# Attention in a two-layer kernel: inverse roots and inverse row sums as exponentials of logarithms

## The chip, the cores and the metric

The program runs on one core of a Trainium2 chip. The metric is the device time of one execution in microseconds. Three executions of the kernel before took 3812.17, 3815.10 and 3818.73 us; the median is 3815.1 us.

## The reference

The input x has 16 batches of 256 tokens with 256 channels. Two layers are added to it in turn. The first runs a shared and a routed feed-forward block, and then a lookup in product keys. The second runs a recurrent cell over the tokens (an LSTM), and then the block that this document is about: attention with 16 heads of 16 channels, and a mixture of 8 experts with two chosen for each token. Cut to this block:

```python
def _layernorm(x, g, b):
    m = jnp.mean(x, axis=-1, keepdims=True)
    v = jnp.mean(jnp.square(x - m), axis=-1, keepdims=True)
    return (x - m) * jax.lax.rsqrt(v + EPS) * g + b
h = _layernorm(x, ln1_g, ln1_b)
q, k, v = jnp.split(h @ w_qkv + b_qkv, 3, axis=-1)          # 16 heads of 16
attn = jax.nn.softmax(einsum('bqhd,bkhd->bhqk', q, k) / np.sqrt(DK), axis=-1)
x = x + einsum('bhqk,bkhd->bqhd', attn, v).reshape(B, S, D) @ w_o + b_o
h = _layernorm(x, ln2_g, ln2_b)
# logits = h @ gate_w + gate_b, the two largest, their softmax as weights,
# relu(h W1 + b1) W2 + b2 of the two experts, added to x with the weights
```

The change concerns three places in it: the inverse root of each of the two norms, and the division by the row sums of the softmax.

## The kernel before

Everything is computed in float32, with channels on the 128 partitions and tokens along the free axis. The attention stage begins at about 2523 us, after the recurrent cell, and works through the 16 batches one by one. A batch passes three generators, which hand over at each `yield`:

- `front(b)`: the first norm (`normed`, lines 1118 to 1140), then the products for queries and keys (L1156, bias and scale on ScalarE at L1159) and for values (L1167, L1169).
- `heads(b)`: four groups `c` of four heads. `largest` multiplies queries and keys (L1190), and takes each row's maximum on VectorE (L1197). `shift` transposes the maxima on TensorE (L1202) and adds them to the queries (L1203). `powers` multiplies again (L1190) and takes Exp on ScalarE (L1209, four of 128x512 for a group). `values` multiplies the powers with the values and with ones (L1220), so that the row sums come out beside the weighted sums; ScalarE copies both into `oT` (L1223).
- `ends(b)`: divides by the row sums (L1242 to L1247), applies the output projection (L1251) and the residual (L1253), runs the second norm (`normed`), adds and stores the sum (L1259 on GpSimd, L1260 a DMA issued by ScalarE's queue), computes the router's logits (L1267), the two choices and their weights (L1269 to L1293, one Exp at L1290), the tokens' rows (L1297 to L1307), their places (L1312 to L1323), four scatters by GpSimd's DMA (L1326), and the list of tiles (L1346 to L1380).

`normed` takes the mean and the variance by products with a matrix of 1/256 (L1122, L1131), so each partition holds the whole mean. In between, VectorE subtracts (L1124) and GpSimd squares (L1126). After the variance come the inverse root (L1133, L1134), the product with it (L1135), and gain and offset (L1137).

Beside them runs `experts()`: tiles of 128 tokens of one expert, 71 in all. A tile is loaded by SyncE (token rows, 1 MB of weights, two biases), transposed (L1413, L1415), multiplied (L1425, in two halves, relu alternately on VectorE at L1431 and ScalarE at L1429), multiplied again (L1438), weighted (L1443), and scattered by GpSimd (L1446). At one time a tile's second product stands between the transposition and the first product of the next.

The order is written out by hand in `drive` (line 1479): `heads(b)` has nine places. At each place one step of `heads(b)` is recorded, then the share of `ends(b - 1)` that falls to it (nine steps over nine places), of `front(b + 1)` (six steps), and of the expert tiles (three pieces to a tile; some 3.6 tiles to a batch once enough tokens have been routed, none in the first batches). After the last batch, `ends(15)` runs over 16 places between tiles, and then the remaining tiles. A layer below the kernel assigns buffers and waits and may move an instruction within its neighbourhood; each engine then runs its own queue in order. Two PSUM buffers (the pool `mm`) serve all of L1122, L1131, L1156, L1167, L1202, L1220, L1251, L1267, L1297 and the small products of the router, in turn. Four others hold the products L1190.

ScalarE keeps one set of function tables at a time. Where the next function is in another set, the build places a table load in front of it; the profile names it ACT_TABLE_LOAD, with the line of that function.

```python
        def drive(main, sides, tiles_from, tiles_to, places):
            a, z = tiles_from * PIECES, tiles_to * PIECES
            for k in range(places):
                steps(main, 1)
                for s, n in sides:
                    steps(s, (k + 1) * n // places - k * n // places)
                go(a + (z - a) * (k + 1) // places)
```

Of the kernel before, what the change touches and what calls it, by code (L numbers as in the profile page):

```python
# [11 lines left out]
AF = mybir.ActivationFunctionType  # L12
ALU = mybir.AluOpType
# [26 lines left out]
def bc(ap, axis, n):  # L40

    a = ap.unsqueeze(axis)
    shape = list(a.shape)
    shape[axis] = n
    return a.to_broadcast(shape)
# [116 lines left out]
def adaln_ffn_kernel(ctx: ExitStack, tc: tile.TileContext, i: dict, out: bass.AP):  # L162
    nc = tc.nc
# [15 lines left out]
    eps = const.tile([P, 1], F32, name="eps")  # L179
# [443 lines left out]
    with tc.tile_pool(name="cw", bufs=1) as cw:  # L623
# [5 lines left out]
        bias = cw.tile([P, 4 * D], F32, name="bias")  # L629
# [369 lines left out]
    QP = QC // 2  # L999
# [3 lines left out]
    with (  # L1003
# [58 lines left out]
        bias = fl.tile([P, 2, QP, 2], F32, name="bias")  # L1062
# [52 lines left out]
        def mm():  # L1115
            return pmm.tile([P, NTT, T], F32, name="mm", tag="mm")

        def normed(x, which, out):

            mean = mm()[:, 0]  # L1120
            for k in range(KC):
                nc.tensor.matmul(mean, ones_d, x[:, k], start=(k == 0), stop=(k == KC - 1))  # L1122
            h = fx.tile([P, KC, T], F32, name=f"h{which}", bufs=2 - which)
            nc.vector.tensor_tensor(h, x, bc(mean, 1, KC), ALU.subtract)  # L1124
            sq = fx.tile([P, KC, T], F32, name="sq", bufs=1)
            nc.gpsimd.tensor_tensor(sq, h, h, ALU.mult)  # L1126
            out.append(h)
            yield
            var = mm()[:, 0]
            for k in range(KC):  # L1130
                nc.tensor.matmul(var, ones_d, sq[:, k], start=(k == 0), stop=(k == KC - 1))  # L1131
            rs = fx.tile([P, T], F32, name="rs", bufs=1)
            nc.scalar.activation(rs, var, AF.Sqrt, bias=eps)  # L1133
            nc.vector.reciprocal(rs, rs)  # L1134
            nc.vector.tensor_tensor(h, h, bc(rs, 1, KC), ALU.mult)  # L1135
            for k in range(KC):
                nc.vector.tensor_scalar(  # L1137
                    h[:, k], h[:, k], lnw[:, 2 * which, k : k + 1], lnw[:, 2 * which + 1, k : k + 1], ALU.mult, ALU.add
                )
            yield  # L1140
# [3 lines left out]
        def front(b):  # L1144

            if b + 1 < B and b > 0:
                load_z(b + 1)
            o = []
            yield from normed(zs[b], 0, o)
            hn = o[0]  # L1150
            qk = qks[b] = fx.tile([P, 2, QC, T], F32, name="qk")
# [87 lines left out]
        def ends(b):  # L1239

            oT, z = outs[b], zs[b]
            rs = fx.tile([P, QP, T], F32, name="rsum", bufs=1)  # L1242
            on = fx.tile([P, QP, T], F32, name="on", bufs=1)
            for h in range(QP):
                nc.vector.reciprocal(rs[:, h], oT[:, h, 1])
                nc.gpsimd.tensor_tensor(on[:, h], oT[:, h, 0], rs[:, h], ALU.mult)
                yield  # L1247
            pw = mm()
            for d in range(KC):
                for k in range(QP):  # L1250
# [5 lines left out]
            yield  # L1256
            o = []
            yield from normed(z, 1, o)
            nc.gpsimd.tensor_tensor(x, x, z, ALU.add)  # L1259
            nc.scalar.dma_start(out=x3d[:, :, b * T : (b + 1) * T], in_=x)  # L1260
# [232 lines left out]
        for b in range(B):  # L1493
            sides = []
            if b:
                sides.append((ends(b - 1), 9))
            if b + 1 < B:
                sides.append((front(b + 1), 6))
            drive(heads(b), sides, planned(b - 1), planned(b), NPL)
        drive(ends(B - 1), [], planned(B - 1), allowed(B - 1), 16)  # L1500
        attn.close()
        pools["first"] = final.enter_context(tc.tile_pool(name="ep2", bufs=2, space=PSUM))
# [102 lines left out]
```

## Time and profile before

| what | us |
|---|---|
| median of three executions | 3815.1 |
| the profiled execution, its own time | 3815.34 |
| its span, from first to last instruction | 3813.4 |
| PE (TensorE, products) busy | 3575.2 |
| DVE (VectorE) busy | 2311.3 |
| ACT (ScalarE) busy | 1278.5 |
| POOL (GpSimd) busy | 698.1 |
| attention stage, first norm to last routing | about 2533 to 3585 |
| inverse of the roots, L1134, 32 times | 56.0 |
| inverse of the row sums, L1245, 32 times | 55.9 |
| table loads at L1133, L1209 and L1290, 64 times | 82.2 |

How to read the lines shown further on: a line of a timeline gives the start, the duration (both in us), the engine, the source line, the operation, what it writes and reads, and in brackets how long the engine had been idle before it and what ended that. A line of groups gives the total busy time and the mean of one in ns, then the idle time before these instructions. PEld is the loading of weights into TensorE. The granted clock is the share of TensorE's full clock that it was given.

### The profile page before, as it was taken

Reading aid. Unit: us, or ns where it says so; the run is one execution under the profiler, and the core shown is the slowest. Engines: PE = TensorE matmul, PEld = TensorE weight load, DVE = VectorE, ACT = ScalarE, POOL = GpSimd, SP = SyncE. Lnnn points to the kernel's source line nnn. Section 1 sums busy time; section 2 is a strip of 40 time slices with the busy share of each in tenths; the row PEclk is TensorE's granted clock in tenths of the full one; section 3 lists DMA queues with packets and bytes.
Section 4 is the critical chain, followed back from the end, with each engine's and each line's share of the span. In section 5 each row is a group of like instructions: output and inputs, shape, how many; then the busy total and the mean of one; then the engine's idle time right before and its main releaser. Section 6 shows DMA issues by size and latency. Waiting matters only on the chain.

```text
span 3813.4 us, 74402 instructions
## 1 busy us (share of the span) xinstructions
PE 3575.2 (94%) x27672; PEld 2820.5 (74%) x27672; DVE 2311.3 (61%) x7704; ACT 1278.5 (34%) x3158; POOL 698.1 (18%) x1148
## 2 busy tenths in 40 slices
PE   7899879999999999999999999959999999999896
PEld 4377468888888888888888888825677777777796
DVE  3333378777777777877777777434554545554323
ACT  1133123333333333333333333323343433433221
POOL 3544310000000000000000100001222222222321
PEclk9999979999999999999999999968899999999997
DMA  6233521011111111011101111040133323232566
GB/s 227 93 106 104 163 34 29 15 34 21 34 21 29 26 29 34 15 34 21 34 18 32 21 32 25 19 127 17 55 98 99 109 86 114 93 113 87 177 225 215
DMA packets 423365, 273.15 MB, mean 72 GB/s; under 512 B 304800, under 2 KB 381472, under 8 KB 412384
## 3 DMA queue, kind: packets, MB, share of 16 engines
q1 hardware_dynamic: 397776, 208.21, 20.3%
q0 software_dynamic: 13344, 36.60, 2.6%
q10 hardware_dynamic: 11888, 23.60, 1.8%
q8 instruction: 223, 3.65, 0.4%
q14 instruction: 134, 1.10, 0.1%
HBM read 191.88 MB, written 76.44 MB: 70 GB/s over the span
## 4 chain that ended last, share of the span: by engine, by line
PE 81%; DVE 6%; DMA 6%; issue 3%; ACT 3%; POOL 2%; SPq 0%; DVEq 0%; ACTq 0%; POOLq 0%
PE acc L819 13%; PE po L810 12%; PE wp L794 12%; PE gp L887 8%; PE g L1438 6%; PE g L1425 5%; PE sc L1190 3%; PE mm L1220 3%; PE bp L843 3%; PE sp L708 3%; PE ph L517 2%; PE py L531 2%; DMA axd<-row,slot 1%; PE mm L1156 1%; PE mm L1251 1%
## 5 line engine op out<-in xcount | busy, mean ns | idle before, releaser
L819 PEld LDWEIGHTS acc<-ge,kout 128*128 128x128 f32 x4096 | 485.2, 192 | 73.8 <-issue 56.9
L810 PEld LDWEIGHTS po<-yt,kin 128*128 128x128 f32 x3840 | 460.9, 192 | 100.7 <-issue 100.7
L819 PE MATMUL acc<-ge,kout 128*128 128x128 f32 x4096 | 522.0, 279 | 2.9 <-DVE ge L816 2.9
L794 PEld LDWEIGHTS wp<-oh,ol 128*128 128x128 f32 x4096 | 494.3, 195 | 28.5 <-issue 24.2
L794 PE MATMUL wp<-oh,ol 128*128 128x64 f32 x4096 | 507.7, 274 | 7.0 <-DVE oh L791 4.0
L810 PE MATMUL po<-yt,kin 128*128 128x128 f32 x3840 | 508.6, 281 | 0.0
L907 POOL TENSOR_SCALAR zt<-hT 128x32 f32<-128x32 f32 x256 | 148.4, 580 | 1606.8 <-DVE hT L906 1439.0
L788 DVE TENSOR_TENSOR ol<-chosen,iota 128x1024 f32<-128x1024 f32 x256 | 315.4, 1232 | 106.2 <-PE wp L794 74.6
L887 PE MATMUL gp<-wh,hT 128*32 128x256 f32 x4096 | 326.9, 393 | 27.7 <-DVE hT L906 18.4
L797 ACT COPY wts<-wp 128x256 f32<-128x256 f32 x512 | 166.6, 375 | 449.9 <-PE wp L794 449.9
L1438 PE MATMUL g<-mw,hT 128*128 x1136 | 280.9, 402 | 9.0 <-ACT hT L1429 3.9
L1425 PE MATMUL g<-xT,w 128*128 128x128 f32 x2272 | 273.6, 276 | 0.0
L1425 PEld LDWEIGHTS g<-xT,w 128*128 128x128 f32 x2272 | 268.8, 192 | 4.4 <-issue 0.3
L1438 PEld LDWEIGHTS g<-mw,hT 128*128 128x128 f32 x1136 | 224.1, 203 | 46.8 <-ACT xT L1415 7.8
L1429 ACT ACTIVATE hT<-g,b 128x128 f32<-128x128 f32 x284 | 104.3, 368 | 437.1 <-DVE hT L1431 371.6
L816 DVE TENSOR_TENSOR ge<-ge,wts 128x512 f32<-128x512 f32 x256 | 175.8, 687 | 88.9 <-ACT ge L815 81.4
L893 ACT ACTIVATE g<-gp 128x192 f32<-128x192 f32 x256 | 84.5, 330 | 424.5 <-PE gp L887 424.5
L815 ACT ACTIVATE ge<-po 128x512 f32<-128x512 f32 x256 | 152.7, 597 | 212.7 <-PE po L810 202.0
L887 PEld LDWEIGHTS gp<-wh,hT 128*32 128x32 f32 x4096 | 120.4, 110 | 127.4 <-issue 27.5
L1190 PE MATMUL sc<-qk 32*128 32x256 f32 x2048 | 199.8, 425 | 14.8 <-DVE npads L1197 10.3
L1431 DVE TENSOR_SCALAR hT<-g,b 128x128 f32<-128x128 f32 x284 | 96.5, 341 | 133.9 <-PE g L1425 82.8
L896 DVE SCALAR_TENSOR_TENSOR fc<-g,cell 128x64 f32<-128x64 f32 x256 | 58.1, 227 | 196.1 <-ACT g L893 194.1
(349 smaller groups left out, 5554.3 us busy)
## 6 DMA issues: line engine op xcount, KB each, us to landing
w<-in_mw SPq DMA_DIRECT2D x71, 1024.0 KB
xwd<-xw SPq DMA_DIRECT2D x64, 256.0 KB
xr<-xwd SPq DMA_DIRECT2D x256, 64.0 KB
xs<-axd SPq DMA_DIRECT2D x71, 129.0 KB
xs<-xsd SPq DMA_DIRECT2D x71, 129.0 KB
b<-in_b SPq DMA_DIRECT2D x71, 128.0 KB
r<-ayd SPq DMA_DIRECT2D x64, 128.0 KB
mw<-in_mw SPq DMA_DIRECT2D x8, 1024.0 KB
```

The lines of the kernel that those rows point to most:

```text
L788: nc.vector.tensor_tensor(ol, bc(c[:, 0, g : g + GT], 2, P), bc(iota, 1, GT), ALU.is_equal)
L794: nc.tensor.matmul(wp[:, t], ol[:, t, :], oh[:, t, :], start=True, stop=True)
L797: nc.scalar.copy(w[:, :, at : at + GT], wp[:, :, r, :].rearrange("p t c -> p c t"))
L810: nc.tensor.matmul(po[:, h, :].rearrange("p (b t) -> p b t", t=SPC), kin[:, k, (c + h) * P : (c + h + 1) * P], yu[:, k], start=(k == 0), s ...
L815: nc.scalar.activation(ge, po, AF.Gelu)
L816: nc.vector.tensor_tensor(ge, ge, w[:, c : c + CQ, :], ALU.mult)
L819: nc.tensor.matmul(acc[d], kout[:, c + h, d * P : (d + 1) * P], ge[:, h, :], start=(c + h == 0), stop=(c + h == NC - 1))
L887: nc.tensor.matmul(gp[j * CW : (j + 1) * CW], state["hT"][:, k, :], group(wh, k, j), start=False, stop=(k == KC - 1), skip_group_check=True,)
L907: nc.gpsimd.tensor_scalar(zt[:, :, :, t], hT[:, :, 0:B], 0.5, None, ALU.mult)
L1190: nc.tensor.matmul(s[j][:, t], qk[rows(j), w, c, t * P : (t + 1) * P], qk[rows(j), 1 - w, c, :], start=True, stop=True)
L1425: nc.tensor.matmul(ph[:, f], w1[n][:, k, at * P : (at + 1) * P], xT[n][:, k], start=(k == 0), stop=(k == KC - 1))
L1438: m = nc.tensor.matmul(acc, hT[n][:, f], mw2[:, bass.ds(e, 1), f].rearrange("p o d -> p (o d)"), start=(f == 0), stop=(f == NF - 1))
```

## The change

In `normed`, ScalarE's Sqrt of the variance and VectorE's reciprocal become a Ln and an Exp with scale -0.5, both on ScalarE. In `ends`, two rounds of a reciprocal on VectorE, a product on GpSimd and a `yield` become one Ln and one Exp with scale -1 over both halves on ScalarE, one product on VectorE, and one `yield`. So `ends` has eight steps where it had nine, while `drive` still deals them out as nine.

```diff
             rs = fx.tile([P, T], F32, name="rs", bufs=1)
-            nc.scalar.activation(rs, var, AF.Sqrt, bias=eps)
-            nc.vector.reciprocal(rs, rs)
+            nc.scalar.activation(rs, var, AF.Ln, bias=eps)
+            nc.scalar.activation(rs, rs, AF.Exp, scale=-0.5)
             nc.vector.tensor_tensor(h, h, bc(rs, 1, KC), ALU.mult)
...
             rs = fx.tile([P, QP, T], F32, name="rsum", bufs=1)
             on = fx.tile([P, QP, T], F32, name="on", bufs=1)
-            for h in range(QP):
-                nc.vector.reciprocal(rs[:, h], oT[:, h, 1])
-                nc.gpsimd.tensor_tensor(on[:, h], oT[:, h, 0], rs[:, h], ALU.mult)
-                yield
+            nc.scalar.activation(rs, oT[:, :, 1], AF.Ln)
+            nc.scalar.activation(rs, rs, AF.Exp, scale=-1.0)
+            nc.vector.tensor_tensor(on, oT[:, :, 0], rs, ALU.mult)
+            yield
             pw = mm()
```

## The prediction

> **What bounds the kernel now.** I read the page's busy row first, then the stages, the waits of the attention stage, and its timeline at the places where PE stood still. The page:
>
> ```profile
> PE 3575.2 (94%) x27672; PEld 2820.5 (74%) x27672; DVE 2311.3 (61%) x7704; ACT 1278.5 (34%) x3158; POOL 698.1 (18%) x1148
> ```
>
> PE is the bound of the program, with 238 us not busy. The changed lines run only from about 2523 us on. The stages by windows (columns: length, then busy us and count of PE, PEld, DVE, ACT, POOL, granted clock, DMA share, GB/s):
>
> ```profile
> 2600.00:2755.00 155.00, 143.92 (x1004) 93.05 (x1005) 80.06 (x208) 60.80 (x107) 29.95 (x51) 0.84 0.11 35
> 2755.00:3541.00 786.00, 740.26 (x6218) 590.73 (x6210) 411.49 (x1107) 306.94 (x625) 201.53 (x289) 0.96 0.31 101
> 3541.00:3600.00 59.00, 48.85 (x313) 43.61 (x306) 21.53 (x74) 12.58 (x31) 18.22 (x22) 0.91 0.47 158
> ```
>
> In the middle stage (twelve batches, with expert tiles between the heads) PE is 94% busy, DVE 52%, ACT 39%. So neither DVE time nor ACT time counts by itself; what counts is PE's 46 us of idling and what ends it. The waits, over 2720 to 3813 us (waiting line, releaser, us in total, times, longest):
>
> ```profile
> PE mm L1267 <- ACT hT L1429: 12.9, 11, 1.7
> PE mm L1202 <- ACT rs L1133: 10.6, 7, 3.5
> PE mm L1360 <- ACT hT L1429: 6.8, 8, 0.9
> ```
>
> L1267 (router logits) is put down to hT, but in the timeline it starts as the normalised h is ready: the last wait is the norm chain. One such place:
>
> ```profile
> 3042.73 1.28 ACT L1209 ACT_TABLE_LOAD   x1
> 3044.02 2.06 ACT L1209 ACTIVATE at<-sc 128x512 f32<-128x512 f32 x4
> ...
> 3046.10 1.28 ACT L1133 ACT_TABLE_LOAD   x1
> ...
> 3047.40 0.47 ACT L1133 ACTIVATE rs<-mm,eps 128x256 f32<-128x256 f32 x1
> ...
> 3047.91 1.75 DVE L1134 RECIPROCAL rs<-rs 128x256 f32<-128x256 f32 x1 [5.60 <-ACT rs L1133]
> ...
> 3047.93 0.44 PE L1202 MATMUL mm<-ident,npads 128*128 128x128 f32 x2 [1.09 <-ACT rs L1133]
> ...
> 3051.18 1.07 PE L1267 MATMUL mm<-w_wg,h 128*128 128x8 f32 x8 [1.74 <-ACT hT L1429]
> ...
> 3052.80 5.31 PE L1438 MATMUL g<-mw,hT 128*128 x16
> ```
>
> Read it as a chain: table load, four Exps, table load, Sqrt (which frees the PSUM buffer that L1202 needs), reciprocal, two DVE steps, logits. PE stands still 1.1 and 1.7 us, and the next L1438 takes 5.31 us where an unstalled one takes 3.62: the clock dropped. Listing PE's timeline from 2755 to 3541, eight batches are of this kind (B). They lose 24.8 us at L1202 and L1267, 6.8 us at L1360, and 14.9 us in slow L1438. Four (A, where L1438 lies between variance and logits) lose only 3.7 us at L1131 and 2.4 us at L1267.
>
> **The change, part by part.** The groups that it touches:
>
> ```profile
> L1134 DVE RECIPROCAL rs<-rs 128x256 f32<-128x256 f32 x32 | 56.0, 1749 | 75.5 <-ACT rs L1133 75.4
> L1245 DVE RECIPROCAL rsum<-oT 128x256 f32<-128x256 f32 x32 | 55.9, 1748 | 28.1 <-ACT oT L1223 28.1
> L1133 ACT ACT_TABLE_LOAD x32 | 41.1, 1283 | 0.6
> L1209 ACT ACT_TABLE_LOAD x19 | 24.4, 1283 | 32.1 <-PE sc L1190 21.9 <-issue 10.0
> L1290 ACT ACT_TABLE_LOAD x13 | 16.7, 1283 | 0.2
> L1133 ACT ACTIVATE rs<-mm,eps 128x256 f32<-128x256 f32 x32 | 15.2, 474 | 16.3 <-PE mm L1131 15.9
> ```
>
> *Engine time.* Removed: 64 reciprocals, 112 us of DVE, and 32 multiplies L1246, 23.5 us of POOL. Added to DVE: 16 multiplies of 128x512 at 0.69 us (row L1135), 11 us. ACT: Ln stands for Sqrt at 0.47. No row shows an Exp of 128x256 from SBUF; a copy of that size from PSUM takes 0.37 (L1415), and SBUF costs some 0.04 more (0.256 at L902 against 0.218 at L894), so between 0.37 and 0.47: I take 0.42, 32 times. Ln and Exp of 128x512: 0.605 (L1209) plus 0.04, between 0.60 and 0.70, I take 0.63, 32 times.
>
> *Table loads.* Here two rules of the Trainium skill speak. Its page "ScalarE: Activation LUTs", section "Table sets: the hidden batching unit", says that one set holds both ln and exp, so the pair needs one load; all the switches of this stage could then go. The built order of the changed kernel says otherwise: a load stands before every Ln and every Exp, 96 in the stage against 64 (32+19+13), and none is left at L1209 and L1290. I go by the built order: 32 x 1.283 = 41 us more on ACT. With one set the place 0 stall below would vanish and the time be about 3770. The same page, section "What ACT_TABLE_LOAD costs", gives about 2.66 us for a switch, a drain of 1.38 included. The rows show 1.28: the four Exps start at 3044.02, where the load from 3042.73 ends. By the page each pair would be 2.76 us longer, at two places in twelve batches 66 us, and the time about 3860. I take the row.
>
> Sum on ACT: 41 + 13 + 20 = 74 us, some 56 of it in the middle stage: 39% becomes 46%, still no bound.
>
> *Order.* Dropping one yield makes ends() eight steps instead of nine. Everything from L1251 on (output projection, z, second norm, logits, routing, four scatters L1326 on POOL, the tile list) comes one place earlier between the heads. Its DMAs: the load of x (SP, L1255) waits for its buffer, which the store L1260 frees; it is issued a place earlier and landed long before use. L1260 on ACT's queue now stands before two hT and the four Exps of the first head group, and waits for L1259 on POOL, which stands before both L1126. The tile list is earlier, which can only help the 5.8 us wait for xs at 3590.
>
> *Place 0, where a wait is added.* After the last values PE goes on as here:
>
> ```profile
> 3015.78 0.58 ACT L1223 COPY oT<-mm 128x512 f32<-128x512 f32 x1 [1.83 <-PE mm L1220]
> ...
> 3018.76 2.48 DVE L1197 TENSOR_REDUCE npads<-sc 128x2 f32<-128x512 f32 x4
> ...
> 3022.40 0.38 PE L1202 MATMUL mm<-ident,npads 128*128 128x128 f32 x2
> ```
>
> In the new DVE order the multiply L1246 stands before these four maxima, and waits for the second activation: oT ends 3016.36, load 3017.65, Ln 3018.3, load 3019.6, Exp 3020.2, multiply 3020.95, maxima 3023.45. L1202 could start at 3022.4 and waits 1.05 us. Behind L1246 on DVE stand the maxima and ys; for the maxima waits PE. If L1438 (3.6 us, the cover here) is missing, as in batches 1 to 3, it is 2.1 us. Next, z is ready 12.6 us after the values' end, L1259 at 13.9, so L1260 leaves ACT before the Exps, whose products end at 15.4: nothing late there.
>
> *The norm places.* PE's new order in B: variance of the front, L1425, L1438, maxima products, variance of ends (ends at 26.0 on the same scale), L1425 2.0, products 1.15, logits. On ACT the load is done before; Ln 26.5, load 27.8, Exp 28.25; DVE 0.69 and 0.73 with hand-over to 29.8. PE arrives at 29.15: 0.65 us of waiting. In A: variance ends at 22.3, but ACT first does the transposed tile and two hT (23.85), then load 25.15, Ln 25.65, load 26.95, Exp 27.4, DVE 28.95; PE arrives at 27.45 after L1438: 1.5 us. L1202 finds its buffer free in both, and L1360 now follows the values (3.6 us), so its wait goes.
>
> *Sum of the middle stage.* B: before 24.8 + 6.8 + 14.9 = 46.5, after 8 x (1.05 + 0.65) = 13.6: 33 less. A: before 6.1, after 4 x 2.55 = 10.2: 4 more. Of the slow-clock part I count half, since the new waits may drop the clock as well: 7.5 back. Net -33 + 4 + 7.5 = -22 us.
>
> *Batches 1 to 3* (no tiles between): by the same walk the first group of Exps comes 3.8 us later, but the last values end 4.4 us sooner, because the reciprocal that held L1203 (1.96 us of PE at 2694) is gone. Between +12 and -13 over the three; I take 0. *Tail:* the 1.8 us wait at 3566 for an hT behind Sqrt goes, one behind L1260 may come: between +2 and -8 with the xs wait; 0. *First norm:* load and Exp (1.70) replace the reciprocal (1.75): 0.
>
> The profiled execution has a span of 3813.4 and took 3815.3, beside a median of 3815.1. 3815 - 22 = **3793 us**.
>
> **The rivals.**
> 1. *ScalarE's chain sets the pace* (slower). L1246 ties DVE's queue to a chain of two loads on ACT ahead of the maxima, in 15 batches, and the clock drops after such waits. For it: L1202 has only 1.1 us of slack left over the maxima even now; in batches 1 to 3 it has none. Against it: DVE and ACT are half idle, and one L1438 covers most of the chain. Price: 15 x 2.4 = 36 us, with half of the gain left (-12): 3839. It decides once the wait per batch passes some 2 us, where the slow L1438 begins to be paid too.
> 2. *The stall only moves*: the norm chain has 4 engine steps before and after, two loads of 1.28 against load and reciprocal; if the earlier place gives no slack, only the 6.8 us at L1360 are saved and the 1.05 x 12 paid: 3815 to 3821, say 3817.
> 3. *The gain comes in full*: the slow clock goes wholly and batches 1 to 3 gain: 3815 - 29 - 13 = 3773.
>
> **How the numbers follow.** A measurement of this kernel tells 0.2% (7.6 us) from no change. Likeliest case and case 3 together 0.58 (its own range 3768 to 3808), case 2 0.12, case 1 0.30. The bounds of the unknown costs (batches 1 to 3 at +-12, tail, clock) make 3768 the low end; with case 1 at 3839 and its spread, 3848 the high end. Faster 0.60, same 0.09, slower 0.31.
>
> **What would show it.** 96 table loads of 1.28 us at L1133, L1134, L1244, L1245, none at L1209. A wait of about 1 us at L1202 for npads once a batch, in the place after L1167; waits of L1267 under 1.5 us; none at L1360; L1438 at 3.6 us after the logits. I am wrong if L1202 or L1251 wait over 2 us in place 0, if the loads take longer than 1.3 us, or if the Exps L1209 wait behind L1260.

## The result and the profile after

The changed kernel took a median of 3844.0 us (3841.5 to 3859.6) against 3815.1 us, a ratio of 1.0082 with a 95% interval of 1.0061 to 1.0104: slower by 29 us between the medians and by 31 us as the ratio. The forecast of 3793 us had the wrong sign; rival 1 had said 3839. The profiled execution has a span of 3841.7 us and took 3844.0.

The busy row of the changed kernel, then the last two of the stretches that the prediction showed of the kernel before (columns as there):

```profile
PE 3570.1 (93%) x27672; PEld 2817.2 (73%) x27672; DVE 2221.5 (58%) x7656; ACT 1350.2 (35%) x3254; POOL 673.5 (18%) x1116
```

```profile
2755.00:3541.00 786.00, 715.52 (x5996) 568.41 (x5993) 333.27 (x1020) 352.34 (x678) 176.87 (x256) 0.96 0.29 97
3541.00:3600.00 59.00, 54.91 (x477) 45.26 (x476) 21.57 (x81) 23.84 (x49) 15.32 (x23) 1.00 0.36 117
```

VectorE fell from 411 to 333 us in the middle stretch and ScalarE rose from 307 to 352, where I had worked out 56 us more (the stretch no longer cuts quite the same work; over the same eleven batches in each kernel, those of the table below, ScalarE goes from 287 to 337). PE, the bound, is busy for 91% of it, where it was 94%. In the last stretch it is busier than before (54.9 against 48.9): its wait for xs there fell from 5.8 to 2.6 us. Its waits from 2720 us on (waiting line, releaser, us in total, times, longest), to be set against the three waits shown of before:

```profile
PE g L1438 <- ACT xT L1415: 21.8, 14, 3.2
PE mm L1267 <- DVE h L1137: 15.2, 10, 2.0
...
PE g L1438 <- ACT hT L1429: 13.3, 5, 3.3
PE mm L1202 <- DVE npads L1197: 10.6, 11, 1.0
...
PE mm L1202 <- DVE where L1364: 8.8, 8, 1.7
```

L1360's wait is gone and L1202 no longer waits for rs, as predicted. In their place stand two waits of L1438, which the prediction did not have, a longer one of L1267, and two new ones of L1202: for the maxima (L1197), and for L1364, a step of the tile list on VectorE. The groups on ScalarE and VectorE that answer to those of before:

```profile
L1133 ACT ACT_TABLE_LOAD x32 | 41.1, 1283 | 36.3 <-PE mm L1131 33.3 <-DVE h L1135 2.6
L1134 ACT ACT_TABLE_LOAD x32 | 41.1, 1283 | 0.6
...
L1244 ACT ACT_TABLE_LOAD x16 | 20.5, 1283 | 0.3
...
L1134 ACT ACTIVATE rs<-rs 128x256 f32<-128x256 f32 x32 | 13.3, 416 | 0.4
...
L1246 DVE TENSOR_TENSOR on<-oT,rsum 128x512 f32<-128x512 f32 x16 | 11.1, 692 | 34.4 <-ACT rsum L1245 34.4
```

The sizes are those of the prediction (1.283, 0.416 and 0.692 us; Ln and Exp of 128x512 take 0.63). What it had not read is in the first row: the loads of L1133 stood idle 33 us for the variance, where in the row of before it is 0.6 in all. No load is left at L1209 and L1290.

One place of kind B, in order of time. PE stands still twice:

```profile
3055.30 1.28 ACT L1133 ACT_TABLE_LOAD   x1
...
3056.60 0.47 ACT L1133 ACTIVATE rs<-mm,eps 128x256 f32<-128x256 f32 x1
...
3057.09 1.28 ACT L1134 ACT_TABLE_LOAD   x1
...
3058.38 0.42 ACT L1134 ACTIVATE rs<-rs 128x256 f32<-128x256 f32 x1
3058.70 0.35 ACT L1415 COPY xT<-g 128x256 f32<-128x256 f32 x1
...
3059.11 5.41 PE L1438 MATMUL g<-mw,hT 128*128 x16 [2.60 <-ACT xT L1415]
...
3065.63 1.13 PE L1131 MATMUL mm<-sq,ones_d 128*128 128x256 f32 x4
...
3066.84 1.28 ACT L1133 ACT_TABLE_LOAD   x1 [5.03 <-PE mm L1131]
3068.14 0.47 ACT L1133 ACTIVATE rs<-mm,eps 128x256 f32<-128x256 f32 x1
...
3068.63 1.28 ACT L1134 ACT_TABLE_LOAD   x1
3069.93 0.42 ACT L1134 ACTIVATE rs<-rs 128x256 f32<-128x256 f32 x1
...
3071.64 1.16 PE L1267 MATMUL mm<-w_wg,h 128*128 128x8 f32 x8 [2.02 <-DVE h L1137]
```

First, load, Ln, load and Exp of the front's norm hold ScalarE from 3055.3 to 3058.8, and the copy of the transposed tile to xT (L1415), which empties a PSUM buffer g, stands behind them; L1438, whose own g comes out of the same two buffers, starts as this copy ends, after 2.60 us of standing still. Second, the load for the norm of ends() begins only when the variance is there (3066.84), so the logits wait 2.02 us. The same place in windows of one microsecond (the number before the DMA share is the granted clock):

```profile
3059.00:3060.00 1.00, 0.89 (x4) 0.81 (x5) 0.96 (x3) 0.06 (x1) 0.00 (x0) 1.00 1.02 401
3060.00:3061.00 1.00, 1.00 (x5) 0.85 (x4) 0.63 (x3) 0.34 (x1) 0.00 (x0) 0.68 0.81 264
3061.00:3062.00 1.00, 1.00 (x4) 0.73 (x3) 0.35 (x1) 0.39 (x2) 0.00 (x0) 0.50 0.11 36
3062.00:3063.00 1.00, 1.00 (x4) 0.81 (x3) 0.00 (x0) 0.00 (x0) 0.00 (x0) 0.50 0.07 16
3063.00:3064.00 1.00, 1.00 (x4) 0.79 (x4) 0.00 (x0) 0.00 (x0) 0.00 (x0) 0.62 0.00 0
```

About a microsecond after PE starts again the clock is granted at half for some 3.4 us, which costs 1.71 us: that is why this L1438 takes 5.41 instead of 3.62. Over the whole middle stage the lost time came in such portions (1.71, 3.42, 5.12). So each kernel's stage can be taken apart: its length, the waits that the timeline puts before PE's instructions, and the clock's loss (one minus the granted clock, summed over windows of half a microsecond). From the first L1167 of batch 4 to that of batch 15, eleven batches, in us:

| kernel | length | waits | lost to the clock | rest |
|---|---|---|---|---|
| before | 719.5 | 39.5 | 29.0 | 651.0 |
| changed | 750.1 | 68.2 | 29.0 | 652.9 |
| norm_only | 720.8 | 54.0 | 17.1 | 649.8 |
| eight_steps | 712.7 | 44.9 | 8.5 | 659.3 |
| sums_only | 735.0 | 49.7 | 22.2 | 663.1 |
| eight_late | 729.9 | 53.0 | 29.0 | 647.9 |
| nine_steps | 728.3 | 59.1 | 20.5 | 648.7 |
| mul_pool | 737.3 | 57.0 | 30.7 | 649.6 |
| rs_two | 747.0 | 60.1 | 23.9 | 663.1 |
| no_norm_loads | 698.2 | 30.9 | 5.1 | 662.2 |
| no_sum_loads | 751.8 | 55.5 | 34.1 | 662.2 |
| one_set | 675.5 | 16.3 | 5.1 | 654.1 |
| norm_one_set | 666.9 | 16.2 | 3.4 | 647.3 |
| one_set_nine | 659.5 | 9.7 | 3.4 | 646.4 |

(The kernels are those of the experiments below. Each row is one profiled execution, and waits under 0.15 us are counted in the rest; the medians are given with each.) For the change itself: the middle stage is 30.6 us longer, 28.7 of it waits. Outside it, the batches 0 to 3 are 2.8 us longer, the part from batch 15 on is 12.4 us shorter, and the attention stage starts 7.3 us later. I do not count the last as an effect of the change: the code ahead of the stage is the same, and two profiles of one and the same kernel (rs_two) have the first L1122 at 2532.7 and 2538.3 us, 5.6 us apart.

### The profile page after: what moved, and what is told of

It reads as the page before. It is cut to its first block, busy times and chain, and to the rows that moved or that the text cites. A ratio compares the mean times of both kernels' runs of the same rounds, so it can differ in the third digit from the quotient of the medians.

```text
span 3841.7 us, 74366 instructions
## 1 busy us (share of the span) xinstructions
PE 3570.1 (93%) x27672; PEld 2817.2 (73%) x27672; DVE 2221.5 (58%) x7656; ACT 1350.2 (35%) x3254; POOL 673.5 (18%) x1116
## 4 chain that ended last, share of the span: by engine, by line
PE 74%; DVE 7%; DMA 7%; ACT 6%; issue 4%; POOL 2%; SPq 1%; ACTq 0%; DVEq 0%; POOLq 0%
PE acc L819 13%; PE po L810 12%; PE wp L794 12%; PE gp L887 8%; PE g L1438 4%; PE g L1425 4%; PE sp L708 3%; PE bp L843 3%; PE sc L1190 3%; PE mm L1220 2%; PE ph L517 2%; PE mm L1156 2%; PE py L531 2%; DVE npads L1197 2%; DMA axd<-row,slot 1%
## 5 line engine op out<-in xcount | busy, mean ns | idle before, releaser
L1438 PE MATMUL g<-mw,hT 128*128 x1136 | 272.7, 395 | 37.0 <-ACT xT L1415 21.8
L1438 PEld LDWEIGHTS g<-mw,hT 128*128 128x128 f32 x1136 | 219.4, 198 | 73.3 <-ACT xT L1415 25.6
L1190 PE MATMUL sc<-qk 32*128 32x256 f32 x2048 | 185.4, 420 | 25.8 <-DVE npads L1197 25.8
L791 DVE TENSOR_TENSOR oh<-oh,chosen 128x512 f32<-128x512 f32 x256 | 174.4, 681 | 3.0
```

The lines of the kernel that those rows point to most:

```text
L791: nc.vector.tensor_tensor(oh, oh, bc(c[:, 2, g : g + GT], 2, 2 * NHI), ALU.mult)
L1190: nc.tensor.matmul(s[j][:, t], qk[rows(j), w, c, t * P : (t + 1) * P], qk[rows(j), 1 - w, c, :], start=True, stop=True)
L1438: m = nc.tensor.matmul(acc, hT[n][:, f], mw2[:, bass.ds(e, 1), f].rearrange("p o d -> p (o d)"), start=(f == 0), stop=(f == NF - 1))
```

## The experiments

Four theories. T1: the loads on ScalarE hold up what PE waits for. T2: the earlier place of everything from L1251 on is to blame. Q: VectorE's queue stands behind the multiply's wait for ScalarE (the tie, for short). T3: the difference arises before the stage. Further letters (L, P, R) are explained where an expectation uses them. Microseconds against before are the ratio and its interval times 3815.

**The parts of the change alone.** norm_only takes only the norms' two lines of the change, sums_only only the row sums' four. nine_steps is the changed kernel with

```diff
             nc.vector.tensor_tensor(on, oT[:, :, 0], rs, ALU.mult)
             yield
+            yield
```

and eight_steps is the kernel before with

```diff
                 nc.gpsimd.tensor_tensor(on[:, h], oT[:, h, 0], rs[:, h], ALU.mult)
-                yield
+            yield
```

> The norms take Ln and Exp as in the changed kernel; the row sums stay with reciprocals on VectorE and multiplies on GpSimd, and ends() keeps nine steps. Table loads in the program stay as before (133). T1 (ScalarE's chain: load, Ln, load, Exp stand ahead of the xT and hT copies on ScalarE, and L1438 waits for these): per norm ScalarE is held 3.5 us instead of 1.8, so waits of L1438 for xT (L1415) appear, of about 1 to 2 us in ten batches, with slow L1438 behind them; about 3825 us. T2 (the earlier place of everything from L1251 on is to blame): order unchanged, so 3815 +- 8. T3 (most of the difference arises before the attention stage and differs between executions): the first L1122 starts between 2533 and 2541 us by chance, the stage itself as before.

> Only the row sums go to Ln and Exp with one multiply (eight steps); the norms stay with Sqrt and reciprocal. T1: at the second norm the table load still waits for nothing new, L1267 waits no longer than before (1.7 us); new are the waits of L1202 for npads (about 1 us per batch) and ScalarE time of 3.8 us per batch at the head of place 0, so the time is 3815 to 3830, and with the norm's share about the 29 us of the whole. T2: the order is that of the changed kernel, so about 3840. My prediction's own sum, had it held, would give some 3795 here.

> The changed kernel with one more yield behind the multiply, so that everything from L1251 on stands in its old place between the heads; ScalarE's work and its 165 table loads stay. T1: 3840 to 3850, since the loads and both pairs are still ahead of xT and hT. T2: back to 3815 +- 8. If the two add up, in between.

> The kernel before (Sqrt, reciprocals, POOL multiplies) with one yield less: everything from L1251 on comes a place earlier, and no Ln or Exp is added. The Sqrts of the front's and the ends' norms become neighbours, 105 table loads instead of 133. T1: faster than before, by 28 loads of 1.28 us where they stood before L1267, and without the wait at L1360: 3785 to 3805. T2: 3835 to 3845. My prediction's order step (the gain is in the order) says about 3790.

Measured: norm_only 1.0004 (0.9993 to 1.0016), +2 us; eight_steps 1.0028 (1.0015 to 1.0041), +11; nine_steps 1.0048 (1.0030 to 1.0066), +18; sums_only 1.0087 (1.0063 to 1.0111), +33; beside +31 for the whole. As they stand, these add up: the row sums' half of the change is the whole loss, and it has two parts: the order (+11 alone; +13 between nine_steps and the changed kernel) and the Ln and Exp of the row sums in the old order (nine_steps over norm_only: +17). In part that is chance. The builds of sums_only and eight_steps have pauses in L1220 (see rs_two below) that the changed kernel, norm_only and nine_steps do not have; in the table the rest of their middle stage is 12 and 8 us longer than before. The profiled execution of sums_only, 11 us over its median, also lost 22 us more to the clock than before in the batches 0 to 3. So the same 31 us do not have the same parts in sums_only and in the changed kernel.

T1 as I had put it failed for the norms: norm_only costs nothing, although its stage shows 19.7 us of new waits of L1438:

```profile
PE mm L1267 <- DVE hT L1431: 19.7, 11, 2.0
PE g L1438 <- ACT xT L1415: 11.2, 7, 1.6
PE g L1438 <- ACT hT L1429: 8.5, 4, 2.1
```

It has as many loads as before, at other places, and what the waits add (14.5 us) the clock gives back (11.9). T2 alone fails too. For the order my prediction had a gain; eight_steps shows why there is none: Sqrt is ready at 3052.6 there, but the reciprocal starts at 3053.46, behind four maxima in VectorE's queue, and L1267 waits up to 2.0 us for the norm. The 29.4 us of waits of before (L1267, L1202 for rs, L1360) became 35.6 (L1267 19.2, L1156 7.4, L1438 9.0); in this profile only the clock gained in the middle stage.

**The multiply's engine, and the order in part.**

```diff
-            nc.vector.tensor_tensor(on, oT[:, :, 0], rs, ALU.mult)
+            nc.gpsimd.tensor_tensor(on, oT[:, :, 0], rs, ALU.mult)
```

for mul_pool, on the changed kernel; for eight_late, on the kernel before,

```diff
-                yield
+                if h == 0 or b < 4:
+                    yield
```

> The changed kernel with the one multiply of the row sums on GpSimd instead of VectorE; loads, Ln and Exp, order and all else stay. Q (VectorE's queue stands behind the multiply's wait for ScalarE): the maxima no longer wait, so the waits of L1202 for npads (9.7 us in the middle stage) and the 13.4 us more of L1190 in the batches without tiles go, and the time is 3820 to 3830. L (the loads hold ScalarE, and what counts is the copies queued there): 3838 or more, since GpSimd's multiply of 128x512 takes longer (about 1.4 us, twice the 0.73 of L1246 before) and L1251 gets its input later.

> The kernel before, with everything from L1251 on one place earlier only from the fifth batch on; the batches without tiles keep the old order. P (the earlier place costs in the batches without tiles, where the profile with eight steps throughout lost 10.7 us at a lower clock, and gains 7 in the middle and 9 at the end): 3797 to 3806, faster than before. R (it costs in the middle as well, and that one profile was a favourable draw): 3815 to 3825.

mul_pool: 3818.7 us, 1.0006 (0.9995 to 1.0016), 25 us under the changed kernel and no longer to be told from before. Its waits of PE in the middle stage:

```profile
PE g L1438 <- ACT xT L1415: 17.8, 7, 3.3
PE mm L1267 <- DVE h L1137: 14.1, 7, 2.0
PE g L1438 <- ACT hT L1429: 12.6, 4, 3.3
PE mm L1202 <- DVE where L1364: 8.1, 7, 1.9
...
PE sc L1190 <- DVE npads L1197: 0.8, 1, 0.8
```

The waits of L1202 for the maxima (9.7 us) are gone, with the same 96 loads and the same order; those of L1190 in the batches without tiles fall from 23.0 to 16.6. This is Q, 1 us under its expectation: the engine of one instruction is worth 25 us by the medians and 29 by the ratios, nearly the whole loss. In the two profiles 12.8 us of it lie in the middle stage (750.1 and 737.3) and 9.4 in the batches 0 to 3 (225.6 and 216.2).

eight_late: 3822.6 us, 1.0009 (0.9997 to 1.0022), not to be told from no change; not the gain that P expected, and inside the range of R. Its profile has 29.0 us lost to the clock in the middle stage, where eight_steps has 8.5, so the clock's gain there does not come with the order by itself. eight_steps has the pauses in L1220 and eight_late has not; whether they are the order's 11 us is not shown.

**Without any table load.** The set that holds both functions is loaded once, by name, before the first Ln:

```diff
+            if "set" not in now:
+                pre = now["set"] = nc.scalar.preload_act_table_set("natural_log_exp_and_others")
+                after_all(tc, pre.ins, [m.ins])
...
             nc.scalar.activation(rs, rs, AF.Exp, scale=-0.5)
```

(`m` is the last product of the variance; lines left out put the Ln behind the load.) one_set is this on the changed kernel, one_set_nine adds the second yield, norm_one_set is the kernel before with the norms alone on Ln and Exp from this set.

> The changed kernel with the one table set that holds both ln and exp loaded once ahead of the stage: none of the 96 table loads is left in it, ScalarE's pairs take 1.3 and 0.9 us instead of 3.8 and 3.5, order and engines stay. L (the loads are what makes the multiply, the maxima behind it and the xT and hT copies late): the waits of L1202 and L1190 for npads fall to those of before, those of L1438 to under 1 us, and with the measured 11 us of the earlier place still paid the time is 3805 to 3820, 25 to 39 us under the changed kernel. Q (the tie itself, a multiply that waits for ScalarE at the head of VectorE's queue, is the price, with or without loads): under 10 us of it goes, 3835 or more. My prediction's own figure for this case was 3770.

> As the kernel with one table set, and one more yield behind the multiply, so that everything from L1251 on stands where it stood before. If the order's price (11 to 13 us in the runs so far) and the loads' price (17 to 22) simply add, this has neither: 3790 to 3808, faster than before by the wait at L1360 or less; if the earlier place only hurt because of what the loads did to ScalarE, it is equal to the one-set kernel with eight steps.

> The kernel before with the norms alone on Ln and Exp, from the one table set that holds both; the row sums stay with reciprocals and GpSimd, in nine steps. No table load is left in the stage, while the kernel with one set for norms and row sums, nine steps too, ran in 3732.7. If the gain of that one was the loads (the norms' and those ahead of the Exps), this is 3725 to 3740, and the row sums' part of the change is worth nothing either way. If the row sums' reciprocals on VectorE still cost what they did (3.9 us at L1190 in the batches without tiles, and VectorE's 56 us), 3745 to 3760.

one_set 3745.6 us, 0.9809 (0.9785 to 0.9832); one_set_nine 3732.7, 0.9776 (0.9748 to 0.9805); norm_one_set 3742.0, 0.9797 (0.9775 to 0.9820). L was right in kind and far too timid, and so was my 3770: taking 96 loads out of the stage gains 98 us. Q failed here: the multiply stands where it stood, and L1202 no longer waits for the maxima at all, so the tie costs only when the Exp that it waits for is late. The two with nine steps beat both kernels, by over 70 us against before; the order's price seems to be there without loads too (13 us, with intervals that overlap). The middle stage of one_set_nine, PE's waits (lines stand 6 or 7 further down in this kernel), then the window of the stage:

```profile
PE mm L1226 <- ACT qk L1165: 3.0, 3, 1.5
PE mm L1131 <- POOL sq L1126: 2.5, 6, 0.4
PE g L1445 <- ACT xT L1422: 2.1, 6, 0.4
...
```

```profile
2751.60:3411.10 659.50, 649.73 (x5717) 524.94 (x5716) 318.58 (x988) 255.92 (x584) 169.54 (x244) 0.99 0.34 111
```

9.7 us of waits instead of 68.2, and a clock of 0.99. Since norm_one_set, with the old reciprocals and GpSimd multiplies, comes within 10 us of it (intervals overlap), the row sums' Ln and Exp are worth little even then; the gain is that neither the norms nor the Exps L1209 need a load. norm_only and norm_one_set have the same order and differ by the 64 loads alone, and the second is 74 us faster. So the kernel before, which has 64 loads too, paid for such loads already: this is a gain to be had, and not what the change cost.

**Single waits.** On the changed kernel, rs_two, xt_dve, and three (these two and mul_pool together):

```diff
-            rs = fx.tile([P, T], F32, name="rs", bufs=1)
+            rs = fx.tile([P, T], F32, name="rs", bufs=2)
```

```diff
-                nc.scalar.copy(xT[n], tp[:, 0:KC])
+                nc.vector.tensor_copy(xT[n], tp[:, 0:KC])
```

> The changed kernel with two buffers for rs instead of one. In the built order of the changed kernel the second norm's Ln has two waits, for the old rs and for the variance, and the one for the variance stands on the table load ahead of it; with two buffers that load has no wait left. If this is why L1267 waits 2.0 us where my working had 0.65, the load runs while the variance is computed and those nine waits of the middle stage fall to about 0.7 (12 us in all), with the slow L1425 or L1438 behind them a little more: 3825 to 3835. If the load starts no earlier because ScalarE is busy until then anyway, nothing moves: 3844 +- 6.

> The changed kernel with the copy of the transposed tile (xT, L1415) on VectorE instead of ScalarE, so that it no longer stands behind the pairs of loads, Ln and Exp. If L1438's waits for xT (18 us in the middle stage, seven places, each with a slow L1438 of some 5.3 instead of 3.6 us behind it) are a true price, about 18 to 25 us go: 3819 to 3826. If PE only pays them in another place (L1202 or L1267, which come right after and need the same ScalarE chain), 3836 or more. The norm change alone had such waits too, 11 us, and cost nothing in the end, which speaks for the second.

> Three edits on the changed kernel together, with all its table loads: the row sums' multiply on GpSimd, two buffers for rs, xT on VectorE. If the waits named are each a price of their own, the parts add up to 25 + 12 + 20: about 3787. If a load's time on ScalarE reaches PE by one way or another, whichever tile is taken out of its queue, no more than 35 go: 3809 or more, still 60 over the kernel without loads (3745.6).

rs_two 3851.2 us, 1.0088 (1.0064 to 1.0113): no gain. Its waits in the middle stage:

```profile
PE g L1438 <- ACT xT L1415: 17.8, 7, 3.3
PE g L1438 <- ACT hT L1429: 12.9, 4, 3.3
...
PE mm L1220 <- issue: 5.3, 12, 0.8
PE mm L1267 <- DVE h L1137: 4.8, 7, 0.7
```

The mechanism is as supposed: with two buffers the loads no longer wait for the variance (0.6 us of idle time before all 32, instead of 36.3), and L1267's waits fall from 14.6 to 4.8 us, the longest from 2.0 to 0.7. But a new row stands there, L1220 put to "issue". PE's timeline in one batch:

```profile
3090.56 1.93 PE L1220 MATMUL mm<-at,v 128*32 128x256 f32 x32
3092.31 0.60 PE L1220 MATMUL mm<-at,sums 128*32 128x256 f32 x5
3093.19 0.62 PE L1220 MATMUL mm<-at,sums 128*32 128x256 f32 x4 [0.27 <-issue]
3094.60 1.56 PE L1220 MATMUL mm<-at,sums 128*32 128x256 f32 x23 [0.79 <-issue]
```

The second half's 32 products, 1.91 us in the changed kernel, take 3.85 here, broken up by pauses that nothing in the profile explains. The second halves over the middle stage, of the changed kernel and of rs_two:

```profile
L1220 PE MATMUL mm<-at,sums 128*32 128x256 f32 x705 | 43.6, 379 | 0.0
L1220 PE MATMUL mm<-at,sums 128*32 128x256 f32 x705 | 54.2, 384 | 5.9 <-issue 5.3
```

With the first halves (47.1 and 49.5 us), L1220 is busy for 103.7 us in the stage instead of 90.7, and the gain is eaten.

xt_dve 3885.6 us, 1.0178 (1.0151 to 1.0205), 42 us worse: the copy now stands in VectorE's queue behind the norm's multiply L1135, which waits for the very same Exp, so L1438's waits for xT grow from 18.1 to 26.5 us. (In one place L1135 stands idle 4.65 us for rs until 3150.35, and the copy runs at 3151.98.) Nothing follows from it about the price of these waits, except that the copy can't be freed by moving it there. three: 3844.9 us, 1.0081 (1.0050 to 1.0112), as slow as the changed kernel and inside the range of its second expectation. The losses of xt_dve (L1438's waits for xT are 26.5 us here too) and the pauses stand against the gain of mul_pool; that a load's time reaches PE whichever tile is taken out of its queue agrees with this, but is not shown by it.

**Which loads.** Identity for Ln in the norms alone (no_norm_loads), and for the row sums alone (no_sum_loads), on the changed kernel; rs_two a second time (rs_two_again); rs_two with nine steps (rs_two_nine). The first two leave a logarithm out, so the values are others, and with them the choice of experts can be; the number of PE's instructions is the same (27672).

```diff
-            nc.scalar.activation(rs, var, AF.Ln, bias=eps)
+            nc.scalar.activation(rs, var, AF.Identity, bias=eps)
```

```diff
-            nc.scalar.activation(rs, oT[:, :, 1], AF.Ln)
+            nc.scalar.activation(rs, oT[:, :, 1], AF.Identity)
```

> The changed kernel with Identity in place of Ln in the norms alone, which leaves the norms' logarithms out: no table is switched at a norm, 32 of the 96 loads are left, those at the row sums. All other instructions and their order stay. If each load has a price of its own (98 us for 96, about 1 us each), 3774 to 3784. If the norms' loads alone hold PE up (they stand ahead of L1438's xT and hT copies and of L1267), 3755 to 3770, and the slow clock behind these waits goes too. If the two kinds only hide behind each other, 3800 or more.

> The changed kernel with Identity in place of Ln for the row sums alone, which leaves their logarithm out: no table is switched at the head of place 0, 64 loads are left, those at the norms. If each load has its own price of about 1 us, 3810 to 3815. If what counts at the row sums is only that the maxima stand behind the multiply in VectorE's queue, this gains what moving the multiply gained (25 us): 3815 to 3822. If the norms' loads alone count, 3838 or more.

> The kernel with two buffers for rs once more, for a second profile. If PE's pauses inside L1220 (about 1.9 us in each of some twelve groups of 64 products, put to no releaser) belong to the build, they are there again at the same groups, and L1220 takes 105 to 109 us in the middle stage; if they belong to that execution, L1220 takes 93 to 95 as in the changed kernel, and the time falls by some 12 us.

> Two buffers for rs in the kernel with nine steps (3831.2), whose profile shows no pauses inside L1220. If the load's wait on the variance has a price that only those pauses hid, L1267's waits fall from 19 to 8 us or less in the middle stage and the time to 3815 to 3823. If PE pays them in another place, 3827 or more.

no_norm_loads: 3787.2 us, 0.9928 (0.9912 to 0.9945), 57 us under the changed kernel, just above the range for an even price per load:

```profile
PE mm L1202 <- DVE npads L1197: 9.7, 10, 1.0
PE mm L1220 <- issue: 8.8, 18, 0.8
...
PE g L1438 <- ACT hT L1429: 2.7, 4, 1.1
PE g L1438 <- ACT xT L1415: 2.5, 6, 0.6
```

L1438's waits fall from 30.7 to 5.2 us, L1267's are gone, and the clock's loss falls from 29.0 to 5.1: the waits named in the timeline above are indeed the norms' loads, and the clock follows the waits. This kernel has the pauses in L1220 too: L1220 is busy for 101.7 us in the stage, 11 more than in the changed kernel, so I estimate the gain without them at 68.

no_sum_loads: 3853.1 us, 1.0110 (1.0086 to 1.0135). Only the third expectation's number holds: L1202's waits for the maxima go as with mul_pool, but L1438's stay, the clock loses 5 us more, the pauses in L1220 come (102.3 us for it here), and nothing is gained. Yet with the norms' loads gone, taking the row sums' away as well gains 42 (from 3787.2 to 3745.6). So the prices don't add: what the row sums' loads cost shows in full only where the norms' are gone. Why mul_pool gains 25 us by freeing the maxima and this kernel nothing is settled in part at most, by the pauses (some 12 us of PE's time in L1220).

rs_two_again: 3852.8 us in one execution, with 101.4 us for L1220 and the pauses in it again, so they belong to the build. rs_two_nine: 3836.9 us, 1.0064 (1.0047 to 1.0081), no faster than nine_steps; L1267's waits stay at 19.2 us there. In the old order the loads of L1133 stood idle 0.6 us with one buffer as with two, where four Exps L1209 lie between the two norms' loads; there was nothing for the second buffer to free. The load that waits for the variance is a thing of the new order, in which two norms follow each other on ScalarE.

## Why the prediction was wrong

**Engine time and table loads: right.** 96 loads of 1.283 us, Ln 0.47 and 0.63, Exp 0.42 and 0.63, the multiply 0.69; ScalarE remains far from being the bound by its time. Of the two rules of the Trainium skill (page "ScalarE: Activation LUTs"), the drain in "What ACT_TABLE_LOAD costs" shows in no row here: Ln starts at 3056.60, the load began at 3055.30. "Table sets: the hidden batching unit" is right that one set holds both functions, and the build does not choose it by itself; my figure for that case, 3770, was 24 us too high, because I let only the stall of place 0 go with the loads (3793 less its 12.6 us is 3780; for the other 10 there was no working). The case that I took was the right one (96 loads), its price the wrong one.

**Place 0: right in size.** L1202 waits 0.97 us for the maxima, ten times, where I had 1.05 in twelve, and mul_pool gains 12.8 us in the middle stage, where I had 12.6. For batches 1 to 3 I took 0 between +12 and -13. The batches 0 to 3 came out 2.8 us longer, though L1190's waits there rose from 13.4 to 23.0 us, two lines of before and one of after:

```profile
PE sc L1190 <- DVE npads L1197: 9.5, 13, 1.5
PE sc L1190 <- DVE qk L1203: 3.9, 2, 2.0
...
PE sc L1190 <- DVE npads L1197: 23.0, 9, 4.6
```

The tie of rival 1, L1246 holding VectorE's queue ahead of the maxima until ScalarE is done, is real: it is what mul_pool takes away. That its 3839 was 5 us off is luck in part. It had 2.4 us in each of 15 batches, where L1202 waited 0.97 us in ten, it kept half of a gain that did not come, and L1438's waits are not in it.

**The norm places: the step that failed.** "On ACT the load is done before" was false. In the built order of the changed kernel the second norm's Ln needs two waits, because rs has one buffer, and the one for the variance stands on the load, once the two norms are neighbours on ScalarE: L1267 waited 2.02 instead of 0.65 us, and rs_two brought it to 0.7. "PE arrives at 29.15" also took L1438 and the tile's copies as independent of ScalarE's order. They are not: xT and hT are copied by ScalarE, behind the pair of the front's norm. That is 30.7 us of waits against 0 in my sum, and no_norm_loads shows that they go when the norms' loads go. For the tile list a place earlier my sum had only a help (the wait for xs did fall), and no price: L1202 waits 8.2 us for L1364 in the middle stage, in seven places, and the waits of before have no such row.

Of the 33 us to be gained in the B batches 16.5 us of waits did go (L1202 for rs, L1360). But my sum let the waits of the middle stage fall by 14 us (37.7 to 23.8), and they rose by 28.7. Of the 43 us between, 30.7 are L1438's, 8.2 L1202's for L1364, and 3.4 L1267's (14.6 where I had 11.2). With the multiply on GpSimd (mul_pool) L1438's waits stay at 30.4 us and the kernel is level with before: these waits eat up the gain, and the tie makes the loss.

**The clock: failed with it.** I counted half of the slow L1438 as gained. The clock lost 29.0 us before and 29.0 after, because slow stretches followed the new waits as they had the old (16 of them, mostly of 3.4 us; before, 9 of 3.4 to 10.2 us).

**The tail and the first norm: set to 0.** The part from batch 15 on is 12.4 us shorter, more than the bound of 8; eight_steps has 8.6 of it (337.9 to 329.3), which speaks for the order.

**Open.** That the waits of L1438 for xT have the price that they show was not tried by itself; norm_only has such waits and loses nothing, because L1202 no longer waits for rs there and the clock gives back the rest. The pauses in L1220 and the order's 11 us are not explained, nor why no_sum_loads gains nothing where mul_pool gains 25 us.

## What to carry to other kernels

When an activation is added to an in-order engine, list every copy that stands behind it in that engine's queue and ask who waits for it: here the cost was not the 74 us of engine time, but two PE waits and a row of maxima. Look in the built order at what the table loads wait for, and if two functions share a table set, ask for that set by name: here this turned a loss of 0.8% into a gain of 1.9%, and norm_one_set had about as much without the row sums' part of the change. Put a multiply that waits for a late engine on a queue in which nothing urgent follows it.

## What was not expected of the hardware

The clock's losses came in equal portions: half clock for 3.413 us, 1.71 us each. In the changed kernel's middle stage 15 of 16 slow stretches began within 2.4 us of the end of a PE wait of 1.6 us or more, but there were 20 such waits. Where a wait lies counts as well. In each of the 18 profiles all slow stretches last whole multiples of 3.413 us and begin on one fixed grid of that period. I cut the attention stage of all profiles into these periods and took those that follow a period at full clock: after a period in which PE was busy for less than 40%, all 117 were slow; after 40 to 60%, 110 of 188; after 95% or more, 11 of 3306. So one and the same wait can cost 1.7 us more or nothing, by how it falls into these periods.

PE paused inside L1220 or the few instructions behind it in seven of the kernels with eight steps (eight_steps, sums_only, rs_two, xt_dve, three, no_norm_loads, no_sum_loads). They have 10 to 24 pauses over 0.2 us in the middle stage that the profile puts to "issue", and L1220 is busy for 100 to 104 us there. The kernels with nine steps, the changed kernel, one_set, mul_pool and eight_late have no such pause, and 89 to 95 us. PE's instructions stand in the same order in rs_two and the changed kernel, so that order is not the cause; and of these pauses, 129 in eight profiles, only two overlap a transfer on the instruction queues (q8, q14), so a fetch of instructions by DMA does not show as the cause either. The pauses shift a build by some 10 us, and any comparison of single edits in this kernel has to be read with them.
